# Centred weights and in-place gates in a four-layer graph network kernel on one Trainium2 core

## The chip, the cores and the metric

The kernel runs on one core of one Trainium2 chip. The metric is the device time of one execution in microseconds (us); the time of a version is the median over its runs. The profile is one execution on the same chip, seen by the hardware profiler. The engines of the core are TensorE (matmuls, called PE in the profile, its weight loads PEld), VectorE (DVE), ScalarE (ACT), GpSimd (POOL) and SyncE (SP), which issues the transfers. PSUM, into which TensorE writes, has eight banks of 128 partitions by 512 float32 values.

## The reference

The input x is 64 x 256 x 128 (batch, node, channel), the adjacency matrix `adj` is 256 x 256; everything is float32. Four layers follow one another, each with a residual and a layer norm without learned scale:

```python
x = _layernorm(x + L0(x))      # sum over k of adj^k x W_k, seven weights, adj given twice
x = _layernorm(x + L1(x))      # adj (x W1) + b1
x = _layernorm(x + L2(x))      # (A_norm x) W2^T + b2, A_norm the normalised adj + I
x = _layernorm(x + L3(x))      # five steps of a gated recurrent unit over the graph

# one step of L3, with h starting as x and in_matrix = out_matrix = adj
m = adj @ h;  av = concat(m, m);  u3 = h @ u3_w.T + u3_b
z = sigmoid(av @ w3_w.T + w3_b + u3)
r = sigmoid(av @ w4_w.T + w4_b + u3)
hv = tanh(av @ w5_w.T + w5_b + (r * h) @ u5_w.T + u5_b)
h = (1 - z) * h + z * hv

# _layernorm(x): (x - mean(x)) / sqrt(var(x) + 1e-5), over the 128 channels
```

## The kernel before

The batch is cut into 32 groups of two (`NB` = 2, L15). A group's values are tiles of 128 partitions by 512 columns: two batch elements times two halves of the nodes times 128 channels. `Group.record` (L648 to L758) writes down what a group does, operation by operation, and nothing is run there: each operation goes into a plan with an engine, an estimated cost, a lag until its result is seen, a rank and the values that it reads and writes. `Plan.order` (L83) then plays the plan through with these estimates. At every step each engine offers the operation that could start first (ties go to the lower rank, that is the earlier group), and the earliest of these offers is placed. Buffers belong to this game: a value takes a slot of its kind when its first operation is placed, and gives it back when its last one has ended. Eight PSUM banks are one such kind (`BANKS` = 8, L24). The resulting list is emitted as it is, so every engine works through a fixed order, and waits on the chip where an operand is late. At most eight groups are in flight (`ACTIVE` = 8), since a group's first operation waits for the last one of the eighth before it.

One-time work is put into the plan by `pre`: the transposed adjacency `aT`, its square, the weights. The four weights of layer 0 are summed from seven by VectorE (`w0_sums`, L277; the identity is added to the first for the residual), `w1s`, `b1s` and `b2s` are loaded as they are (L352 to L356), and `transposed` (L364) turns the 128x128 weights on TensorE and copies them out of PSUM on ScalarE.

A group goes through these stages:

- Layer 0: x times the squared adjacency (`propagate`, L672), products with the summed weights into two banks `py0`, `v` copied out, `aT` times `v` added, the sum copied to SBUF by ScalarE as `s0` (L699).
- A norm: `statistics` (L455) takes bn_stats and bn_aggr and two small scalings on VectorE (L461 to L468), the power and one product on GpSimd (L471, L472), and `normalise` (L484) applies scale and bias in four ScalarE instructions (L489).
- Layers 1 and 2: GpSimd adds the bias to the residual (`yb`, L711), `propagate` multiplies with the adjacency, a weight product goes into `py`, VectorE adds `yb` (L481), and the norm follows.
- Layer 3, five steps (L729): `propagate`, then the products of m and of hT with the gate weights. `pr` is the bank of the gates r and z: u3 hT + w4 m gives r, and w34 m added later turns the same bank into the pre-activation of z. `ph` is the bank of the candidate: w5 m + u5 (r hT). ScalarE does the gates (`gate_`, L636), VectorE does rh, d = hv - hT, e = z d and hT + e (`tensor`, L643), then a transpose and a round trip through DRAM bring h back into the other layout (`packed`, L616).
- The last residual and norm 3, then the output. The last four groups take the transpose on TensorE (L754 to L756).

`propagate` for a full group is the scheme `seven` (L510): seven block products in place of eight, with three subtractions on GpSimd before (L531 to L538), a copy on ScalarE in between (L572) and four additions on VectorE (L559 to L569) whose results gate the later block products of TensorE, since these overwrite parts of the bank that the additions read.

All matmuls are recorded under the helper at L198, all plain VectorE operations of a step under L645. Float32 matmuls are split in two instructions by the compiler, so a product counts as x2 in the profile.

Of the kernel before, what the change touches and what calls it, by code (L numbers as in the profile page):

```python
# [9 lines left out]
AF = mybir.ActivationFunctionType  # L10
OP = mybir.AluOpType
AX = mybir.AxisListType

P = 128
# [8 lines left out]
EPS = 1e-5  # L23
# [120 lines left out]
def pe_cost(columns, n=1):  # L144
    return n * 2 * (max(columns, P) / 1.2 + 2)
# [6 lines left out]
def act_cost(elements):  # L152
    return elements / 1.2 + 165
# [3 lines left out]
def kernel(  # L157
# [30 lines left out]
    nc = tc.nc  # L188
    B, N, C = x.shape
# [7 lines left out]
    def mm(o, lhsT, rhs, start, stop, shared=False):  # L197
        nc.tensor.matmul(o, lhsT, rhs, start=start, stop=stop, skip_group_check=shared)  # L198
# [7 lines left out]
    def constant(name, shape):  # L206
        v = Val("const", shape, name)
        v.tile = const.tile(shape, F32, name=name)
        return v

    def temp(name):
        return Val("bank", SHAPES["bank"], name)

    def pre(rank, engine, cost, run, reads=(), writes=()):
        lag = {"SP": 2300, "PE": 260, "DVE": 260, "ACT": 130, "POOL": 100}[engine]
        plan.add(engine, cost, lag, rank, run, reads, writes)

    def load(rank, name, shape, src, keep=True):
        v = constant(name, shape) if keep else Val("w", shape, name)
        pre(rank, "SP", 450, lambda: nc.sync.dma_start(v.ap, src), [], [v])  # L220
        return v

    ident = const.tile([P, P], F32, name="ident")
    make_identity(nc, ident)
    half = const.tile([P, Q], F32, name="half")
# [18 lines left out]
    aT, a2T = constant("aT", [P, T, N]), constant("a2T", [P, T, N])  # L244
# [30 lines left out]
    w0s = constant("w0s", [P, 4, C])  # L275
# [6 lines left out]
    pre(-7, "DVE", 1300, w0_sums, [w0_raw], [w0s])  # L282


    w0p = constant("w0p", [P, 2, C])

    def permuted():
# [15 lines left out]
    ahat, anT = Val("w", [P, T, N], "ahat"), constant("anT", [P, T, N])  # L303
# [27 lines left out]
    def block_sums(rank, name, aTs):  # L331
# [3 lines left out]
        def run():  # L335
# [13 lines left out]

    w1s = load(1.3, "w1s", [P, C], w1)  # L352
    b1s = load(1.4, "b1s", [P, C], bass.AP(tensor=b1.tensor, offset=b1.offset, ap=[[0, P], [1, C]]))
    raw = {name: load(1.5, f"raw_{name}", [P, src.shape[1]], src, False)
           for name, src in (("w2", w2), ("w4", w4_w), ("w3", w3_w), ("w5", w5_w), ("u3", u3_w), ("u5", u5_w))}
    b2s = load(1.5, "b2s", [P, C], bass.AP(tensor=b2.tensor, offset=b2.offset, ap=[[0, P], [1, C]]))  # L356
    both = {name: Val("w", [P, C], f"both_{name}") for name in ("w4", "w3", "w5", "w34")}
    for name in ("w4", "w3", "w5"):
        pre(0.4, "DVE", 220, lambda o=both[name], i=raw[name]: nc.vector.tensor_add(
# [1 line left out]
    pre(0.4, "DVE", 220, lambda: nc.vector.tensor_sub(both["w34"].ap, both["w3"].ap, both["w4"].ap),  # L361
        [both["w3"], both["w4"]], [both["w34"]])

    def transposed(name, *parts_):  # L364
        ps, v = temp(f"p_{name}"), constant(name, [P, len(parts_) * P])

        def run():
            for i, src in enumerate(parts_):
                nc.tensor.transpose(ps.ap[:, i * P:(i + 1) * P], src.ap, ident)

        n = len(parts_) * P
        pre(0.4, "PE", len(parts_) * 110, run, parts_, [ps])
        pre(0.4, "ACT", act_cost(n), lambda: nc.scalar.copy(v.ap, ps.ap[:, :n]), [ps], [v])
        return [(v, v.ap[:, i * P:(i + 1) * P]) for i in range(len(parts_))]

    w2T, u3T = transposed("w2u3T", raw["w2"], raw["u3"])
    w4T, w34T, w5T, u5T = transposed("w435u5T", both["w4"], both["w34"], both["w5"], raw["u5"])

# [8 lines left out]
    zb, rb, hb = ((bsum, bsum.ap[:, i:i + 1]) for i in range(3))  # L387


    def nat(v):  # L390
        return v.ap.rearrange("p (q c) -> p q c", c=C)
# [21 lines left out]
    class Group:  # L413
# [41 lines left out]
        def statistics(self, tag, s):  # L455
            st, mv, ve, rs, nm = (self.val(k, n + tag) for k, n in (
                ("st", "st"), ("mv", "mv"), ("ve", "ve"), ("rs", "rs"), ("ve", "nm")))

            def stats():
                for q in range(self.q):  # L460
                    nc.vector.bn_stats(st.ap[:, q * 6:(q + 1) * 6], nat(s)[:, q, :])  # L461

            def aggr():
                for q in range(self.q):
                    nc.vector.bn_aggr(mv.ap[:, 2 * q:2 * q + 2], st.ap[:, q * 6:(q + 1) * 6])
                mean, var = (mv.ap.rearrange("p (q k) -> p k q", k=2)[:, k] for k in range(2))
                nc.vector.tensor_scalar(ve.ap, var, EPS, None, op0=OP.add)
                nc.vector.tensor_scalar(nm.ap, mean, -1.0, None, op0=OP.mult)  # L468

            def scales():  # L470
                nc.gpsimd.tensor_tensor(rs.ap, ve.ap, half[:, :self.q], op=OP.pow)  # L471
                nc.gpsimd.tensor_tensor(mv.ap[:, :self.q], nm.ap, rs.ap, op=OP.mult)  # L472

            self.dve(stats, [s], [st], 195 * self.q)
            self.dve(aggr, [st], [mv, ve, nm], 67 * self.q + 240)
            self.add("POOL", 1420, 100, scales, [ve, nm], [rs, mv])
            return mv, rs

        def residual(self, tag, ps, resid, left=lambda v: v.ap, right=lambda v: v.ap):
            s = self.val("w", "s" + tag)  # L480
# [152 lines left out]
        def product(self, ps, w, rhs, start, stop, shared=False):  # L633
            self.pe(pe_cost(self.width), lambda: mm(ps.ap, w[1], rhs.ap, start, stop, shared), [rhs, w[0]], [ps])

        def gate_(self, name, ps, func, bias):  # L636
            t = self.val("w", name)
            self.act(lambda: nc.scalar.activation(t.ap, ps.ap, func, bias=bias[1], scale=1.0),  # L638
                     [ps, bias[0]], [t],
                     act_cost(self.width) + 100)  # L640
            return t
# [6 lines left out]
        def record(self):  # L648
# [24 lines left out]
            v, s0 = self.val("w", "v"), self.val("w", "s0")  # L673
            py = []
# [16 lines left out]
            for t in range(T):  # L691
# [9 lines left out]

                self.pe(pe_cost(self.nb * C, T), second, [v, aT], [py[t]])
                self.act(summed, [py[t]], [s0], act_cost(self.nb * C))
            y = self.normalise("0", s0, *self.statistics("0", s0))


            for tag, ats, w, bias in (("1", aT, (w1s, w1s.ap), b1s), ("2", anT, w2T, b2s)):
                yb = self.val("w", "yb" + tag)

                def biased(yb=yb, y=y, bias=bias):  # L710
                    nc.gpsimd.tensor_tensor(nat(yb), nat(y), bias.ap[:, None, :].to_broadcast([P, self.q, C]),  # L711
                                            op=OP.add)

                self.add("POOL", 40 + 625 * self.nb, 100, biased, [y, bias], [yb])
                m = self.propagate(tag, y, ats)
                py = self.val("bank", "py" + tag)

                def weight(py=py, m=m, w=w):
                    for q in range(self.q):
                        mm(py.ap[:, q * P:(q + 1) * P], m.ap[:, q * P:(q + 1) * P], w[1], True, True)  # L720

                self.pe(pe_cost(P, self.q), weight, [m, w[0]], [py])
                y = self.normalise(tag, *self.residual(tag, py, yb))


            h = y
            hT = self.brought("hT", self.turned("h", h, "p (q k j) -> p q k j", "p (k q i) -> p q k i"))
            ats, ins = aT, None
            for s in range(STEPS):  # L729
                m = self.propagate(f"g{s}", h, ats, ins, True)  # L730
                pr = self.val("bank", f"pr{s}")
                self.product(pr, u3T, hT, True, False)
                self.product(pr, w4T, m, False, True)
                r = self.gate_(f"r{s}", pr, AF.Sigmoid, rb)
                rh = self.tensor(f"rh{s}", OP.mult, r, hT)
                ph = self.val("bank", f"ph{s}")
                self.product(ph, w5T, m, True, False)
                self.product(pr, w34T, m, False, True, shared=True)
                z = self.gate_(f"z{s}", pr, AF.Sigmoid, zb)
                self.product(ph, u5T, rh, False, True)  # L740
                hv = self.gate_(f"hv{s}", ph, AF.Tanh, hb)

                d = self.tensor(f"d{s}", OP.subtract, hv, hT)
                e = self.tensor(f"e{s}", OP.mult, z, d)
                if s < STEPS - 1:
                    hT = self.tensor(f"hT{s}", OP.add, hT, e)
                    h, ats, ins = self.packed(f"h{s}", hT), aTp, pairs
            if self.start < B - END:
                hT = self.tensor("hT", OP.add, hT, e)
# [75 lines left out]
```

## Time and profile before

The time is 1392.04 us, the median of three runs (1391.99 to 1392.26); the profiled execution has a span of 1389.6 us. Busy time, share and number of instructions of each engine are in the first part of the profile's page. What matters around the change, from the page's groups of instructions (busy time is the union of their spans, mean is that of one instruction):

| group | count | busy us | mean ns |
|---|---|---|---|
| products of m with w4 and w34 into pr (PE, 128x512) | 640 | 325.0 | 597 |
| products of hT with u3 into pr (PE, 128x512) | 320 | 163.4 | 598 |
| bn_stats (DVE L461) | 512 | 110.5 | 275 |
| bn_aggr (DVE L465) | 512 | 46.7 | 151 |
| small scalings of a norm (DVE L467, L468) | 128 each | 32.2, 21.5 | 252, 168 |
| power of a norm (POOL L471) | 128 | 143.7 | 1123 |
| product of a norm (POOL L472) | 128 | 33.9 | 265 |
| normalise (ACT L489) | 512 | 210.6 | 483 |
| r, z, hv (ACT L638) | 160 each | 109.6, 109.5, 109.2 | 685 |
| rh, d, e, hT (DVE L645) | 160 each | 125.9, 122.5, 121.4, 125.6 | 787, 766, 761, 788 |
| residual add of layers 1 and 2 (DVE L481) | 64 | 43.5 | 679 |

A line of a group gives the program line, engine and operation, then output <- inputs by the program's names with buffer numbers left out, the shapes and the count. A line of the waits gives who waited, for whom, and in all how many us, how often, and the longest. A line of the timeline gives the start, the duration, the engine and the operation. A line of the stage table gives, for a stretch of the span, the busy us and the number of instructions of PE, PEld, DVE, ACT and POOL, then the clock that TensorE was granted (1.00 is full), the share of the transfer engines and GB/s.

### The profile page before, as it was taken

To read this page: it belongs to the slowest core of one execution; us is meant where nothing else is said; L and a number is where in the kernel's file an instruction comes from. 1 tells how busy PE (TensorE), PEld (TensorE's weight loads), DVE (VectorE), ACT (ScalarE), POOL (GpSimd) and SP (SyncE) were. 2 spreads that over 40 slices of the span, in tenths; PEclk is the share of its full clock that TensorE was granted. 3 is DMA by queue.
4 is the path that set the end of the run, shared out by engine and by line. 5 is a ranking of instruction groups with operands and counts; after the bars stand their busy time and mean duration, and the time that the engine had idled before them with its cause. 6 is when DMAs were issued, how large, how long until landed. Compare 5 with 4: busy or idle time off the path is not lost.

```text
span 1389.6 us, 22166 instructions
## 1 busy us (share of the span) xinstructions
PE 1347.1 (97%) x6516; PEld 928.3 (67%) x6516; DVE 1114.0 (80%) x3288; ACT 691.1 (50%) x1638; POOL 754.7 (54%) x1089
## 2 busy tenths in 40 slices
PE   8999999999999999999999999999999999899996
PEld 7976656676666766666577775666766667665663
DVE  5678779788887798888778798788888777988776
ACT  3554445455454445545455554544555444554444
POOL 4776526475564474754267575636655435853332
PEclk9999999999999999999999999999999999999998
DMA  6112225333343342433433323343333332133232
GB/s 190 33 54 84 84 69 167 100 98 100 91 115 91 101 113 72 131 88 117 117 87 104 93 77 91 92 128 101 91 115 107 91 90 71 52 124 104 87 91 61
DMA packets 269672, 134.45 MB, mean 97 GB/s; under 512 B 176368, under 2 KB 241392, under 8 KB 269552
## 3 DMA queue, kind: packets, MB, share of 16 engines
q1 hardware_dynamic: 269552, 133.03, 33.0%
q8 instruction: 53, 0.87, 0.3%
q14 instruction: 67, 0.55, 0.1%
HBM read 67.05 MB, written 65.54 MB: 95 GB/s over the span
## 4 chain that ended last, share of the span: by engine, by line
PE 82%; DVE 13%; issue 2%; ACT 2%; DMA 1%; SPq 1%; DVEq 0%; POOL 0%; ACTq 0%; POOLq 0%
PE pr L198 27%; PE ph L198 18%; PE pmg L198 16%; PE py L198 13%; PE pm L198 6%; PE pmq L198 2%; DVE hT L645 2%; DVE d L645 2%; DVE e L645 2%; DVE st L461 1%; DVE s L481 1%; DMA x<-in_x_dram 1%; DVE rh L645 1%; ACT hv L638 1%; DVE th L620 1%
## 5 line engine op out<-in xcount | busy, mean ns | idle before, releaser
L198 PE MATMUL pr<-mg,w435u5T 128*128 128x512 f32 x640 | 325.0, 597 | 2.3 <-DVE mg L569 2.2
L471 POOL TENSOR_TENSOR rs<-ve,half 128x4 f32<-128x4 f32 x128 | 143.7, 1123 | 232.8 <-DVE nm L468 230.7
L531 POOL TENSOR_TENSOR tsg<-h 128x256 f32<-128x256 f32 x128 | 105.2, 822 | 253.5 <-DMA h<-dh 187.6
L489 ACT ACTIVATE y<-s,mv,rs 128x128 f32<-128x128 f32 x512 | 210.6, 483 | 44.1 <-POOL mv L472 42.7
L638 ACT ACTIVATE z<-pr,bsum 128x512 f32<-128x512 f32 x160 | 109.5, 685 | 127.2 <-PE pr L198 125.0
L645 DVE TENSOR_TENSOR rh<-r,hT 128x512 f32<-128x512 f32 x160 | 125.9, 787 | 53.7 <-ACT r L638 52.8
L198 PE MATMUL pr<-hT,w2u3T 128*128 128x512 f32 x320 | 163.4, 598 | 4.2 <-DVE hT L645 3.3
L645 DVE TENSOR_TENSOR d<-hv,hT 128x512 f32<-128x512 f32 x160 | 122.5, 766 | 55.0 <-ACT hv L638 54.2
L198 PE MATMUL ph<-rh,w435u5T 128*128 128x512 f32 x320 | 163.5, 596 | 2.0 <-DVE rh L645 1.9
L638 ACT ACTIVATE r<-pr,bsum 128x512 f32<-128x512 f32 x160 | 109.6, 685 | 109.4 <-PE pr L198 109.1
L198 PE MATMUL ph<-mg,w435u5T 128*128 128x512 f32 x320 | 163.6, 593 | 0.0
L198 PEld LDWEIGHTS pr<-mg,w435u5T 128*128 128x128 f32 x640 | 110.2, 191 | 76.9 <-issue 59.1
L638 ACT ACTIVATE hv<-ph,bsum 128x512 f32<-128x512 f32 x160 | 109.2, 685 | 48.5 <-PE ph L198 47.9
L645 DVE TENSOR_TENSOR hT<-hT,e 128x512 f32<-128x512 f32 x160 | 125.6, 788 | 1.4
L198 PEld LDWEIGHTS pmg<-aTp,h 128*128 128x128 f32 x512 | 88.6, 197 | 52.7 <-issue 38.3
L198 PEld LDWEIGHTS pmg<-s_aTp,tsg 128*128 128x128 f32 x768 | 101.8, 191 | 32.2 <-issue 26.1
L645 DVE TENSOR_TENSOR e<-z,d 128x512 f32<-128x512 f32 x160 | 121.4, 761 | 1.4
L461 DVE BATCH_NORM_STATS2 st<-s 128x6 f32<-128x128 f32 x512 | 110.5, 275 | 3.6 <-ACT s L699 3.0
L198 PE MATMUL pmg<-s_aTp,tsg 128*128 128x128 f32 x768 | 106.5, 275 | 0.2 <-POOL tsg L535 0.2
L581 ACT COPY mg<-pmg 128x128 f32<-128x128 f32 x160 | 42.3, 264 | 121.6 <-PE pmg L198 90.4
L198 PE MATMUL pmg<-aTp,h 128*128 128x128 f32 x512 | 98.7, 280 | 0.5 <-DVE mq L569 0.3
L198 PEld LDWEIGHTS ph<-mg,w435u5T 128*128 128x128 f32 x320 | 58.0, 192 | 57.4 <-issue 41.6
(159 smaller groups left out, 2686.6 us busy)
## 6 DMA issues: line engine op xcount, KB each, us to landing
dh<-th SPq DMA_DIRECT2D x160, 256.0 KB, 2.0
h<-dh SPq DMA_DIRECT2D x256, 128.0 KB, 2.5
x<-in_x_dram SPq DMA_DIRECT2D x32, 256.0 KB, 3.4
hT<-dh SPq DMA_DIRECT2D x128, 64.0 KB, 2.0
out_dram<-y SPq DMA_DIRECT2D x32, 256.0 KB, 2.4
dx<-tx SPq DMA_DIRECT2D x30, 256.0 KB, 2.6
xT<-dx SPq DMA_DIRECT2D x60, 128.0 KB, 2.6
dn<-tn SPq DMA_DIRECT2D x28, 256.0 KB, 2.0
```

What stands on the lines that cost most here:

```text
L198: nc.tensor.matmul(o, lhsT, rhs, start=start, stop=stop, skip_group_check=shared)
L461: nc.vector.bn_stats(st.ap[:, q * 6:(q + 1) * 6], nat(s)[:, q, :])
L471: nc.gpsimd.tensor_tensor(rs.ap, ve.ap, half[:, :self.q], op=OP.pow)
L481: self.dve(lambda: nc.vector.tensor_add(right(s), left(ps), right(resid)), [ps, resid], [s])
L489: nc.scalar.activation(nat(y)[:, q, :], nat(s)[:, q, :], AF.Identity, bias=mv.ap[:, q:q + 1], scale=rs.ap[:, q:q + 1])
L531: nc.gpsimd.tensor_tensor(ts.ap[:, :2 * P].rearrange("p (x c) -> p x c", x=2), ins(h)[:, 1], ins(h)[:, :, 0], op=OP.subtract)
L581: self.act(lambda: nc.scalar.copy(o(m, 0), o(ps, 0, False)), [ps], [m], act_cost(P), True)
L620: self.dve(lambda: nc.vector.transpose(turn.ap.rearrange("p (u j t) -> p u t j", t=T, j=32), src.ap.rearrange("p (u t i) -> p u t i", t=T, ...
L638: self.act(lambda: nc.scalar.activation(t.ap, ps.ap, func, bias=bias[1], scale=1.0), [ps, bias[0]], [t], act_cost(self.width) + 100)
L645: self.dve(lambda: nc.vector.tensor_tensor(out(t), way(a), way(b), op=op), [a, b], [t])
```

## The change

Layers 0 to 2 end in sums whose mean over the channels is to be zero, so that their norms need no mean. For that, each weight has the mean over its output channels taken out once, at the start: the summed weights of layer 0 with the identity (`centre(w0s, w0m)`), w1, b1 and b2 (put together in one tile `wb`), and w2, whose transpose on TensorE becomes a product with the identity less 1/128 everywhere (`less`). The residual that layers 1 and 2 add is a norm's output, which has mean zero already. These norms are then: ScalarE squares and sums the row with its accumulator output (the factor 1/128 sits in the scale), GpSimd adds epsilon and takes the power, and one VectorE multiply with the row factors broadcast gives the output. Norm 3 stays as it was.

In layer 3, z and tanh are written in place into their PSUM banks `pr` and `ph` instead of to SBUF, and d and e read them there. The product of w4 with m is the first one into `pr`, and that of u3 with hT the second.

```diff
+    def centre(v, means):
+        nc.vector.reduce_sum(means.ap, v.ap, axis=AX.X)
+        nc.vector.tensor_scalar(means.ap, means.ap, -1.0 / C, None, op0=OP.mult)
+        nc.vector.tensor_tensor(v.ap, v.ap, means.ap[:, :, None].to_broadcast(v.ap.shape), op=OP.add)
+
+    w0m = constant("w0m", [P, 4])
+    pre(-7, "DVE", 1500, lambda: centre(w0s, w0m), [w0s], [w0s, w0m])
...
-    w1s = load(1.3, "w1s", [P, C], w1)
-    b1s = load(1.4, "b1s", [P, C], bass.AP(tensor=b1.tensor, offset=b1.offset, ap=[[0, P], [1, C]]))
+    wb, wbm = constant("wb", [P, 3, C]), constant("wbm", [P, 3])
+    pre(1.3, "SP", 450, lambda: nc.sync.dma_start(wb.ap[:, 0, :], w1), [], [wb])
+    for i, b in ((1, b1), (2, b2)):
+        pre(1.4, "SP", 450, lambda i=i, b=b: nc.sync.dma_start(
+            wb.ap[:, i, :], bass.AP(tensor=b.tensor, offset=b.offset, ap=[[0, P], [1, C]])), [wb], [wb])
+    pre(0.35, "DVE", 1100, lambda: centre(wb, wbm), [wb], [wb, wbm])
...
+    less = constant("less", [P, P])
+    pre(0.4, "DVE", 200, lambda: nc.vector.tensor_scalar(less.ap, ident, -1.0 / C, None, op0=OP.add), [], [less])
...
-                nc.tensor.transpose(ps.ap[:, i * P:(i + 1) * P], src.ap, ident)
+                if src is raw["w2"]:
+                    mm(ps.ap[:, i * P:(i + 1) * P], src.ap, less.ap, True, True)
+                else:
+                    nc.tensor.transpose(ps.ap[:, i * P:(i + 1) * P], src.ap, ident)
...
+            def squares():
+                for q in range(self.q):
+                    nc.scalar.activation(nat(y)[:, q, :], nat(s)[:, q, :], AF.Square, scale=C ** -0.5,
+                                         accum_out=ve.ap[:, q:q + 1])
+
+            def scales():
+                nc.gpsimd.tensor_scalar(ve.ap, ve.ap, EPS, None, op0=OP.add)
+                nc.gpsimd.tensor_tensor(rs.ap, ve.ap, half[:, :self.q], op=OP.pow)
+
+            self.act(squares, [s], [y, ve], 400 * self.q)
+            self.add("POOL", 1330, 100, scales, [ve], [ve, rs])
+            return y, rs
+
+        def normalise_centred(self, tag, s):
+            y, rs = self.spread_of(tag, s)
+            self.dve(lambda: nc.vector.tensor_tensor(nat(y), nat(s), rs.ap[:, :, None].to_broadcast([P, self.q, C]),
+                                                     op=OP.mult), [s, rs], [y])
+            return y
...
-            t = self.val("w", name)
+            t = self.val("w", name) if kept else ps
...
-            y = self.normalise("0", s0, *self.statistics("0", s0))
+            y = self.normalise_centred("0", s0)
...
-                y = self.normalise(tag, *self.residual(tag, py, yb))
+                y = self.normalise_centred(tag, self.added(tag, py, yb))
...
-                self.product(pr, u3T, hT, True, False)
-                self.product(pr, w4T, m, False, True)
+                self.product(pr, w4T, m, True, False)
+                self.product(pr, u3T, hT, False, True)
...
-                z = self.gate_(f"z{s}", pr, AF.Sigmoid, zb)
+                z = self.gate_(f"z{s}", pr, AF.Sigmoid, zb, False)
                 self.product(ph, u5T, rh, False, True)
-                hv = self.gate_(f"hv{s}", ph, AF.Tanh, hb)
+                hv = self.gate_(f"hv{s}", ph, AF.Tanh, hb, False)
```

More of the change, by code (lines that the diff above doesn't have):

```diff
@@ L348 @@
     block_sums(0.7, "aTp", aTp)
-    w1s = load(1.3, "w1s", [P, C], w1)
-    b1s = load(1.4, "b1s", [P, C], bass.AP(tensor=b1.tensor, offset=b1.offset, ap=[[0, P], [1, C]]))
+    wb, wbm = constant("wb", [P, 3, C]), constant("wbm", [P, 3])
[4 more added lines that the diff above has]
+    pre(0.35, "DVE", 1100, lambda: centre(wb, wbm), [wb], [wb, wbm])
+    w1c, b1c, b2c = ((wb, wb.ap[:, i, :]) for i in range(3))
     raw = {name: load(1.5, f"raw_{name}", [P, src.shape[1]], src, False)
            for name, src in (("w2", w2), ("w4", w4_w), ("w3", w3_w), ("w5", w5_w), ("u3", u3_w), ("u5", u5_w))}
-    b2s = load(1.5, "b2s", [P, C], bass.AP(tensor=b2.tensor, offset=b2.offset, ap=[[0, P], [1, C]]))
     both = {name: Val("w", [P, C], f"both_{name}") for name in ("w4", "w3", "w5", "w34")}
@@ L368, in run @@
             for i, src in enumerate(parts_):
-                nc.tensor.transpose(ps.ap[:, i * P:(i + 1) * P], src.ap, ident)
+                if src is raw["w2"]:
+                    mm(ps.ap[:, i * P:(i + 1) * P], src.ap, less.ap, True, True)
+                else:
+                    nc.tensor.transpose(ps.ap[:, i * P:(i + 1) * P], src.ap, ident)
         n = len(parts_) * P
-        pre(0.4, "PE", len(parts_) * 110, run, parts_, [ps])
+        pre(0.4, "PE", len(parts_) * 110, run, [*parts_, less], [ps])
         pre(0.4, "ACT", act_cost(n), lambda: nc.scalar.copy(v.ap, ps.ap[:, :n]), [ps], [v])
@@ L477, in statistics, with spread_of, added @@
             return mv, rs
+        def spread_of(self, tag, s):
+            y, ve, rs = self.val("w", "y" + tag), self.val("ve", "ve" + tag), self.val("rs", "rs" + tag)
+            def squares():
[13 more added lines that the diff above has]
+            return y
+        def added(self, tag, ps, resid):
+            s = self.val("w", "s" + tag)
+            self.dve(lambda: nc.vector.tensor_add(s.ap, ps.ap, resid.ap), [ps, resid], [s])
+            return s
         def residual(self, tag, ps, resid, left=lambda v: v.ap, right=lambda v: v.ap):
@@ L634, in product, with gate_ @@
             self.pe(pe_cost(self.width), lambda: mm(ps.ap, w[1], rhs.ap, start, stop, shared), [rhs, w[0]], [ps])
-        def gate_(self, name, ps, func, bias):
-            t = self.val("w", name)
+        def gate_(self, name, ps, func, bias, kept=True):
+            t = self.val("w", name) if kept else ps
             self.act(lambda: nc.scalar.activation(t.ap, ps.ap, func, bias=bias[1], scale=1.0),
@@ L703, in record @@
                 self.act(summed, [py[t]], [s0], act_cost(self.nb * C))
-            y = self.normalise("0", s0, *self.statistics("0", s0))
-            for tag, ats, w, bias in (("1", aT, (w1s, w1s.ap), b1s), ("2", anT, w2T, b2s)):
+            y = self.normalise_centred("0", s0)
+            for tag, ats, w, bias in (("1", aT, w1c, b1c), ("2", anT, w2T, b2c)):
                 yb = self.val("w", "yb" + tag)
                 def biased(yb=yb, y=y, bias=bias):
-                    nc.gpsimd.tensor_tensor(nat(yb), nat(y), bias.ap[:, None, :].to_broadcast([P, self.q, C]),
+                    nc.gpsimd.tensor_tensor(nat(yb), nat(y), bias[1][:, None, :].to_broadcast([P, self.q, C]),
                                             op=OP.add)
-                self.add("POOL", 40 + 625 * self.nb, 100, biased, [y, bias], [yb])
+                self.add("POOL", 40 + 625 * self.nb, 100, biased, [y, bias[0]], [yb])
                 m = self.propagate(tag, y, ats)
```

## The prediction

> **What bounds the kernel now.** I read the page's busy times and its chain of waits first, then the waits of the matmul queue, then the matmuls in order of time, and last the groups of VectorE and ScalarE. The page's first and fourth parts:
>
> ```profile
> PE 1347.1 (97%) x6516; PEld 928.3 (67%) x6516; DVE 1114.0 (80%) x3288; ACT 691.1 (50%) x1638; POOL 754.7 (54%) x1089
> ...
> PE 82%; DVE 13%; issue 2%; ACT 2%; DMA 1%; SPq 1%; DVEq 0%; POOL 0%; ACTq 0%; POOLq 0%
> ```
>
> TensorE (PE) is the bound, and what is on the chain beside it is VectorE (DVE). But 97% overstates it, because the shown end of a matmul overlaps the next one. The timeline around 607 us shows how fast full-width products really follow each other:
>
> ```profile
> 607.33 1.02 PE L198 MATMUL ph<-mg,w435u5T 128*128 128x512 f32 x2
> 608.19 1.02 PE L198 MATMUL pr<-mg,w435u5T 128*128 128x512 f32 x2
> 609.04 1.02 PE L198 MATMUL ph<-rh,w435u5T 128*128 128x512 f32 x2
> ```
>
> A pair is shown as 1.02 us and the next pair starts after 0.855, so one 512-wide matmul takes 0.4277 us of the array. In the same way 256-wide ones are 0.2165 apart (36.01, 36.45, 36.88) and 128-wide ones 0.1105. Then PE's own work is 1600 x 0.4277 + 792 x 0.2165 + 4124 x 0.1105 = 684 + 171 + 456 = 1311 us. Walking the matmul starts with these spacings, PE stands still for 59.5 us: 9.1 in the first 50 us, 44.6 between 50 and 1350, 5.8 after that. The other 19 us of the span are 9 after the last matmul and some 10 of slower clock and small gaps. The change touches no matmul count, so only these 78 us can move, and the middle 44.6 are the prize. The waits of the matmul queue say who ends them:
>
> ```profile
> PE pth L591 <- DVE hT L645: 5.2, 2, 4.6
> PE pmg L198 <- DVE mg L565: 5.2, 8, 2.1
> PE pr L198 <- DVE hT L645: 3.3, 6, 1.2
> PE py L198 <- DVE m L569: 2.8, 2, 1.8
> PE pm L198 <- DVE m L565: 2.6, 2, 2.2
> PE pmq L198 <- DMA x<-in_x_dram: 2.4, 2, 1.3
> PE pr L198 <- DVE mg L569: 2.2, 6, 0.6
> ```
>
> Except for the start's x transfer it is VectorE every time: an operation that PE needs stands late in VectorE's queue. The stalls come in clumps, as the stage table shows; where they clump the clock also drops to 0.97:
>
> ```profile
> 300.00:350.00 50.00, 47.93 (x230) 32.07 (x229) 41.82 (x123) 25.62 (x60) 29.59 (x43) 0.97 0.32 92
> 1000.00:1050.00 50.00, 50.00 (x242) 34.56 (x241) 42.43 (x118) 26.48 (x63) 28.67 (x38) 1.00 0.30 90
> 1200.00:1250.00 50.00, 45.98 (x231) 31.57 (x231) 45.48 (x161) 27.62 (x66) 31.29 (x48) 0.97 0.33 106
> ```
>
> **What the skill says.** (1) The Trainium skill, "SBUF — State Buffer", Who interferes with whom: a VectorE instruction with two SBUF inputs contends with a GpSimd instruction that reads SBUF, one with at most one SBUF input does not. The trace agrees: the lines of residual adds and of gate differences (min/median/max ns) are
>
> ```profile
> L481 DVE TENSOR_TENSOR s<-py,yb x64: 645/680/693, 43.5 to 1226.3; 128x512 f32<-128x512 f32 x64
> L645 DVE TENSOR_TENSOR d<-hv,hT x160: 639/692/1598, 84.4 to 1377.5; 128x512 f32<-128x512 f32 x160
> ```
>
> The add with one PSUM input never exceeds 693 ns; the difference with two SBUF inputs reaches 1598. (2) "ScalarE: Activation LUTs", What happens when an `exp` ACTIVATE runs: PSUM is the lower-latency destination for ScalarE. No row before writes PSUM from ScalarE. (3) The same page, What ACT_TABLE_LOAD costs: 186 ns plus 0.833 per element, 93 ns for each pointer operand, back to back 93 less. For the present normalise (two pointers, 128 elements) that gives 479 and a spacing of 386; the trace has 483 and 210.6/512 = 411.
>
> **The change, part by part.**
>
> *Norms 0 to 2 (96 of 128).* Removed from VectorE, as three quarters of the rows' busy time: bn_stats 110.5, aggregates 46.7, the two small scalings 32.2 and 21.5, together 210.9 x 0.75 = 158 us. Added: 96 multiplies of 128x512 with two SBUF inputs, 0.775 each (the rows rh, hT, d and e have 761 to 788) = 74. Net -84 us. ScalarE loses 0.75 x 210.6 = 158 us and gets 384 squares. From below, one pointer operand and a free accumulator: 0.30 each by the page's price; from above, the accumulator as a second instruction with the fixed 186 ns again and less overlap: 0.60. So 115 to 230; I take 0.45 = 173. ScalarE then stands at 650 to 765 us, 47 to 55% of the span: not the bound. GpSimd swaps a 265 ns multiply for an addition on the same 128x4: nothing.
>
> *z and tanh left in PSUM (L645's d and e).* Both now have one PSUM input, so 0.679 as for the add above: 122.5 + 121.4 - 2 x 160 x 0.679 = -27 us. ScalarE's two gates take 685 or somewhat less. Together VectorE goes from 1114 to about 1004 us.
>
> *A new wait.* The multiply stands in VectorE's queue and waits for GpSimd's power; until now it was ScalarE's normalise that waited there (42.7 us over 128 norms, 38 times). If VectorE inherits it, 0.75 x 42.7 = 32 us are blocked, and queued behind are the additions of the seven-product scheme (L559 to L569), for which PE waits. Counting it as load: (1004 + 32)/1375 = 75% against 80%.
>
> *Banks.* From the mean times of opening and closing, pr is held for 17.8 us now (from u3's product to the end of z) and ph for 4.95. Opened by w4's product some 13 us later (about 739.2 against 726.3) and kept to the end of e (748.1, instead of 744.1), pr is held for 9; ph, kept to the end of d, for 6. In mean banks: pr 2.05 to 1.03, ph 0.57 to 0.69, and all kinds together 5.75 to 4.85 of 8. Room is gained even though two values stay longer.
>
> *u3 after w4.* The same two products, but both are now behind m and before r: 0.86 us more on the chain of each step, and 160 x 0.86 = 138 us of PE work that could fill a gap before m was there now cannot. Eight groups are in flight, with 5.8 us of PE work a step each, so in the middle it is hidden behind other groups' products; at the end I charge 1 us.
>
> *The start.* Centring w0 adds three VectorE instructions (0.69 for a 128x512 reduction, 0.17, 0.7) before the first use of w0s at 14.19 us; w0s is ready at 8.9 us, so up to 5 us of slack hides it. Centring b1, b2 and w1 likewise lies before 30.9 us, where b1 is first read. The w2 transpose becomes a matmul of the same width. The tail keeps the old norm 3. I charge 1 us.
>
> *Sum.* If stalls behind a queue grow as load/(1 - load), 80.2% gives 4.05 and 75.3% gives 3.05, a quarter less: 44.6 x 0.25 = -11. Fewer clumps: -2 of clock. Banks: -3, the stalls that no VectorE operation ends (2.1 on "issue", 0.9 on tanh). Start and end +2. In all -14: 1392 - 14 = 1378 us.
>
> **The rivals.** *A, 55%: as summed, 1378*, with some 12 either way, since the planner writes a new order from new costs. *B, 18%: nothing to speak of, 1389.* For it: stall and VectorE load go badly together in the stage table (42.43 busy without stall, 41.82 with 4 us), so the written order, not the load, may set the stalls; then only the clock and a few waits of banks move. Against: the waits name VectorE. *C, 17%: slower, 1402.* The fill work of u3 is gone, the inherited wait blocks the additions, and ScalarE at the upper bound delays its copies: a tenth of 138 us unfilled is +14, half of the 32 us blocked would reach PE as +16, less the -15 to -20 of lighter VectorE and banks: +10. If Square were not in the table in use, loads would come with each norm and this case would be worse; the trace shows one load for sigmoid, tanh, copy and identity. *D, 10%: nearly all middle stalls go, 1350*: 1392 - 40 - 2. For it: contention falls too, and with it the long rows of 1.6 us that start clumps.
>
> **How the numbers follow.** 1378 is A's. The range runs from D's to C's, 1350 to 1403; it leaves out the worse half of C and a little below D. Faster by over 0.2% (below 1389.3): nearly all of A, D, half of B = 0.72; within: 0.08; slower: C and the rest of B = 0.20.
>
> **What would show it.** Right: VectorE near 1005 us busy, d and e at 0.68 with no row over 0.75, fewer waits of PE on hT and L565, no window at 0.97, pr open for about 9 us. Wrong: more than one table load; squares over 0.6 apart; long waits of the new multiply on GpSimd with waits of PE on L559 to L569 behind them; waits of PE on w4's or u3's operands that are longer than now.

## The result and the profile after

The changed kernel takes 1370.02 us (median of 4 runs, 1369.68 to 1371.42) against 1392.15 us of the kernel before in the same session: a ratio of 0.9842, 95% interval 0.9825 to 0.9859. That is 22.1 us less, where 14 were forecast; the time lies in the range. (The kernel before is run again beside each change, so its median differs a little from one comparison to the next.) The profiled span fell from 1389.6 to 1367.9 us.

The engines' busy times and the chain of waits of the changed kernel, to be held against the first two lines that the prediction shows:

```profile
PE 1340.5 (98%) x6517; PEld 926.0 (68%) x6517; DVE 1021.9 (75%) x2431; ACT 650.7 (48%) x2022; POOL 720.4 (53%) x1089
...
PE 91%; DVE 5%; DMA 1%; ACT 1%; issue 1%; POOL 1%; SPq 0%; DVEq 0%; ACTq 0%; POOLq 0%
```

TensorE's share of the chain rose from 82 to 91% and VectorE's fell from 13 to 5%. VectorE is busy 92 us less, ScalarE 40 us less, GpSimd 34 us less. TensorE's own work is the same: with the spacings of the prediction it is 1311.6 us, against 1311.5. Going through the matmul starts in order, and counting as standing still what lies between a start and the one before it beyond these spacings, shows where the time came from:

| TensorE stands still | before, us | after, us |
|---|---|---|
| first 50 us | 9.1 | 9.1 |
| from 50 to 1340 us | 44.6 | 22.9 |
| after that, before the last matmul | 5.8 | 5.9 |
| span left after the start of the last matmul | 8.8 | 8.6 |

The whole gain is 21.7 us of stalls in the middle. Of the 44.6 us before, some 24 are ended by VectorE in the timeline's own records; of the 22.9 after, 9.3 are. The rest mostly are short gaps without a named releaser. In the kernel before, 3.4 us of it are no waits at all but matmuls at half the clock, which the section on new orders below shows; the changed kernel has none of these in the middle. The waits of the matmul queue say the same:

```profile
PE pth L640 <- DVE mv L485: 3.5, 2, 3.2
PE pr L198 <- DVE mg L618: 2.8, 5, 1.0
PE pm L198 <- DVE m L614: 2.3, 3, 1.6
PE pmq L198 <- DMA x<-in_x_dram: 2.0, 1, 2.0
PE ph L198 <- DVE rh L695: 1.9, 4, 0.7
PE warm L238 <- POOL ident masks.py:199: 1.3, 1, 1.3
PE pmg L198 <- ACT usg L621: 0.9, 2, 0.5
```

The waits for `hT` before u3's product (3.3 us) are gone, those for the third addition of the seven-product scheme in layer 3 (`mg` L565 before, 5.2 us) are nearly gone; the wait of the last transpose belongs to the tail and stays. In the stage table the clumps at these places and the two middle windows at clock 0.97 are gone too (the largest idle share in the middle is now 2.7 us, from 1150 to 1200 us); the same three stretches now read

```profile
300.00:350.00 50.00, 49.87 (x261) 36.83 (x260) 34.85 (x87) 23.57 (x80) 30.92 (x49) 1.00 0.33 95
...
1000.00:1050.00 50.00, 49.93 (x231) 34.15 (x230) 38.47 (x97) 22.03 (x68) 32.53 (x50) 1.00 0.37 107
...
1200.00:1250.00 50.00, 48.63 (x198) 28.35 (x198) 39.60 (x95) 23.39 (x53) 15.43 (x25) 1.00 0.36 104
```

d and e, which read tanh and z from PSUM, have lost their long rows, and the new multiply `y`, with two SBUF inputs, has them (min/median/max ns):

```profile
L695 DVE TENSOR_TENSOR d<-ph,hT x160: 644/691/694, 84.5 to 1355.5; 128x512 f32<-128x512 f32 x160
L695 DVE TENSOR_TENSOR e<-pr,d x160: 644/684/693, 85.3 to 1356.7; 128x512 f32<-128x512 f32 x160
L519 DVE TENSOR_TENSOR y<-s,rs x96: 643/691/1774, 28.1 to 1206.2; 128x512 f32<-128x512 f32 x96
```

ScalarE's rows of the new norm and of the two gates in place (count, then busy us and mean ns) are

```profile
L505 ACT ACTIVATE y<-s 128x128 f32<-128x128 f32 x384 | 113.7, 301 | 24.0 <-DVE s L525 23.6
...
L688 ACT ACTIVATE pr<-pr,bsum 128x512 f32<-128x512 f32 x160 | 105.6, 660 | 117.7 <-PE pr L198 114.9 <-DVE d L695 1.1 <-DVE th L669 1.0
L688 ACT ACTIVATE ph<-ph,bsum 128x512 f32<-128x512 f32 x160 | 105.5, 659 | 63.3 <-PE ph L198 62.3 <-DVE mg L618 0.6
L505 ACT ACTIVATION_READ_ACCUMULATOR y<-s 128x1 f32 x384 | 73.2, 191 | 0.0
```

The sum comes out by an instruction of its own, 191 ns, so a square with its sum takes (113.7 + 73.2)/384 = 0.487 us of ScalarE.

### The profile page after: what moved, and what is told of

Same layout as the page of the kernel before. It is cut to its first block, busy times and chain, and to the rows that moved or that the text cites. A ratio compares the mean times of both kernels' runs of the same rounds, so it can differ in the third digit from the quotient of the medians.

```text
span 1367.9 us, 21546 instructions
## 1 busy us (share of the span) xinstructions
PE 1340.5 (98%) x6517; PEld 926.0 (68%) x6517; DVE 1021.9 (75%) x2431; ACT 650.7 (48%) x2022; POOL 720.4 (53%) x1089
## 4 chain that ended last, share of the span: by engine, by line
PE 91%; DVE 5%; DMA 1%; ACT 1%; issue 1%; POOL 1%; SPq 0%; DVEq 0%; ACTq 0%; POOLq 0%
PE pr L198 29%; PE ph L198 19%; PE pmg L198 18%; PE py L198 15%; PE pm L198 6%; PE pmq L198 3%; DVE rh L695 1%; DVE st L481 0%; DMA w_raw<-in_L_gnn_weight_dram 0%; DVE d L695 0%; DVE e L695 0%; DVE s L530 0%; DVE hT L695 0%; ACT r L688 0%; DVE y L519 0%
## 5 line engine op out<-in xcount | busy, mean ns | idle before, releaser
L580 POOL TENSOR_TENSOR tsg<-h 128x256 f32<-128x256 f32 x128 | 102.4, 800 | 256.2 <-DMA h<-dh 157.6
L695 DVE TENSOR_TENSOR d<-ph,hT 128x512 f32<-128x512 f32 x160 | 109.6, 685 | 71.3 <-ACT ph L688 70.4
L688 ACT ACTIVATE pr<-pr,bsum 128x512 f32<-128x512 f32 x160 | 105.6, 660 | 117.7 <-PE pr L198 114.9
L688 ACT ACTIVATE ph<-ph,bsum 128x512 f32<-128x512 f32 x160 | 105.5, 659 | 63.3 <-PE ph L198 62.3
L505 ACT ACTIVATE y<-s 128x128 f32<-128x128 f32 x384 | 113.7, 301 | 24.0 <-DVE s L525 23.6
L695 DVE TENSOR_TENSOR hT<-hT,e 128x512 f32<-128x512 f32 x160 | 119.4, 749 | 1.2
L491 POOL TENSOR_TENSOR rs<-ve,half 128x4 f32<-128x4 f32 x32 | 34.5, 1079 | 151.2 <-DVE nm L488 151.0
L695 DVE TENSOR_TENSOR e<-pr,d 128x512 f32<-128x512 f32 x160 | 108.9, 682 | 1.3
L510 POOL TENSOR_TENSOR rs<-ve,half 128x4 f32<-128x4 f32 x96 | 102.0, 1063 | 8.0
L618 DVE TENSOR_TENSOR mg<-pmg,usg 128x256 f32<-128x256 f32 x160 | 66.8, 418 | 46.4 <-PE pmg L198 45.3
L761 POOL TENSOR_TENSOR yb<-y,wb 128x512 f32<-128x512 f32 x64 | 86.7, 1357 | 26.9 <-DVE y L519 26.9
```

The lines of the kernel that those rows point to most:

```text
L505: nc.scalar.activation(nat(y)[:, q, :], nat(s)[:, q, :], AF.Square, scale=C ** -0.5, accum_out=ve.ap[:, q:q + 1])
L580: nc.gpsimd.tensor_tensor(ts.ap[:, :2 * P].rearrange("p (x c) -> p x c", x=2), ins(h)[:, 1], ins(h)[:, :, 0], op=OP.subtract)
L618: nc.vector.tensor_tensor(o(m, slice(1, 3)), o(ps, slice(1, 3), False), both, op=OP.add)
L695: self.dve(lambda: nc.vector.tensor_tensor(out(t), way(a), way(b), op=op), [a, b], [t])
L761: nc.gpsimd.tensor_tensor(nat(yb), nat(y), bias[1][:, None, :].to_broadcast([P, self.q, C]), op=OP.add)
```

## The experiments

Three theories stand against each other. **Load**: TensorE's middle stalls follow VectorE's load, so what counts is how much work VectorE is spared. **Banks**: what counts is the PSUM room from opening `pr` by w4's product. **Order**: the planner writes a new order for every change, and this one happened to fall well. All ratios are to the kernel before, run beside each kernel (its medians were 1390.4 to 1391.4 us); the changed kernel's own ratio is 0.9842.

### The same order, with VectorE's load put back

```diff
+    idle = const.tile([P, Q * 6], F32, name="idle")
...
+            def multiplied():
+                nc.vector.tensor_tensor(nat(y), nat(s), rs.ap[:, :, None].to_broadcast([P, self.q, C]), op=OP.mult)
+                for q in range(self.q):
+                    nc.vector.bn_stats(idle[:, q * 6:(q + 1) * 6], nat(s)[:, q, :])
+
+            self.dve(multiplied, [s, rs], [y])
```

The plan's costs are untouched, so every engine runs the changed kernel's instructions in the changed kernel's order (the two traces agree in this instruction by instruction), with 384 bn_stats more on VectorE.

> The changed kernel with every engine's order kept as it is, but with four bn_stats more behind each of the 96 multiplies of norms 0 to 2, whose output nobody reads (the outputs of the kernel are the same). VectorE gets back 96 x 4 x 0.216 = 83 us, so its load returns to about 1105 us. Load theory (the stalls of TensorE follow VectorE's load; the change took 92 us from VectorE and 21 us from the middle stalls, 0.23 us for each): about 1389 us. Bank theory (the gain is PSUM room, from opening pr by w4's product): below 1375. Order theory (each new plan falls out differently, and this one fell well): below 1375, since the order is the same.

Measured: 1389.47 us, ratio 0.9989 (0.9983 to 0.9995). The busy times and the added group in this kernel:

```profile
PE 1347.6 (97%) x6517; PEld 926.4 (67%) x6517; DVE 1086.3 (78%) x2815; ACT 649.9 (47%) x2022; POOL 717.9 (52%) x1089
```

```profile
L523 DVE BATCH_NORM_STATS2 idle<-s 128x6 f32<-128x128 f32 x384 | 82.7, 275 | 0.0
```

82.7 us of idle work on VectorE, 64 in its busy time, cost 19.4 us, with every order, bank and buffer the same. The middle stalls went from 22.9 to 41.9 us, none of them at a lowered clock. GpSimd is as busy as in the changed kernel (718 us against 720), and the readers of `y` don't wait for the idle work: GpSimd's addition to `y` (L761) starts 0.28 us after the multiply's end in the median of both kernels. So it is the operations queued behind that come late. The load theory named 1389 and the other two below 1375. This is the main finding: VectorE work of about the size that the change takes away has a price of the size of the gain. The idle work stands in 96 blocks behind the multiplies, not where the removed work stood; that the same load costs the same in other places isn't shown.

### The same order, with the gates' results in SBUF

```diff
-            t = self.val("w", name) if kept else ps
+            t = self.val("w", name)
...
-                     [ps, bias[0]], [t],
+                     [ps, bias[0]], [t] if kept else [t, ps],
...
-                d = self.tensor(f"d{s}", OP.subtract, hv, hT)
-                e = self.tensor(f"e{s}", OP.mult, z, d)
+                d = self.tensor(f"d{s}", OP.subtract, hv, hT, held=[ph])
+                e = self.tensor(f"e{s}", OP.mult, z, d, held=[pr])
```

The plan believes the banks to be held as in the changed kernel, so the order is the same instruction by instruction, as the traces confirm.

> The changed kernel with z and tanh written to SBUF again, but the plan told that their banks stay held until d and e have ended, so that every engine keeps its order. Only d and e change: two SBUF inputs, which meet GpSimd's reads. Load theory: VectorE gets some 25 us more and rows beyond 1 us, about 1376 us. Bank and order theory: 1370 within 2.

Measured: 1382.61 us, ratio 0.9939 (0.9923 to 0.9955). The busy times and the row of d:

```profile
PE 1345.8 (97%) x6517; PEld 927.7 (67%) x6517; DVE 1052.3 (76%) x2431; ACT 657.4 (48%) x2022; POOL 772.1 (56%) x1089
```

```profile
L695 DVE TENSOR_TENSOR d<-hv,hT x160: 642/692/1767, 86.9 to 1368.7; 128x512 f32<-128x512 f32 x160
```

The long rows are back, and 12.6 us with them, about twice what VectorE's load alone led me to expect. The load theory has the sign; what it lacked is the other side of the meeting: GpSimd, which does the same operations in both kernels, is busy 52 us longer (720.4 against 772.1). Its middle subtraction of layer 3, in the changed kernel first and in this one second, takes 547 and 640 ns in the mean:

```profile
L584 POOL TENSOR_TENSOR tsg<-h,tsg 128x128 f32<-128x128 f32 x128 | 69.8, 547 | 5.9
...
L584 POOL TENSOR_TENSOR tsg<-h,tsg 128x128 f32<-128x128 f32 x128 | 81.7, 640 | 5.9
```

So two SBUF inputs in d and e slow both engines that feed TensorE, and waits of TensorE for a GpSimd subtraction now appear (1.1 us). ScalarE's two gates are some 25 ns longer each as well, since they write to SBUF. How the 12.6 us divide between the three engines wasn't separated. In the profiled execution 2.4 us of the difference stand in the first 50 us, where TensorE waits 3.3 us for x instead of 2.0, and 10.9 in the middle.

### One part taken out of the changed kernel

Each of these three lets the planner write a new order. (Where the old norms are put back, here and below, the weights stay centred.)

```diff
-            y = self.normalise_centred("0", s0)
+            y = self.normalise("0", s0, *self.statistics("0", s0))
...
-                y = self.normalise_centred(tag, self.added(tag, py, yb))
+                y = self.normalise(tag, *self.residual(tag, py, yb))
```

> The changed kernel with the old norm (bn_stats, aggregates, four scalings on ScalarE) in layers 0 to 2; the weights stay centred. VectorE gets back some 70 us. Load theory: 1370 + 0.23 x 70 = 1386 us. Bank theory: 1370 to 1374. Order theory: anywhere from 1365 to 1395.

```diff
-                z = self.gate_(f"z{s}", pr, AF.Sigmoid, zb, False)
+                z = self.gate_(f"z{s}", pr, AF.Sigmoid, zb)
...
-                hv = self.gate_(f"hv{s}", ph, AF.Tanh, hb, False)
+                hv = self.gate_(f"hv{s}", ph, AF.Tanh, hb)
```

> The changed kernel with z and tanh in SBUF as before, so that the plan gives pr and ph back early and writes its own order. Against the run with the gates in SBUF and the order kept (1382.6), this one has more room in PSUM and VectorE the same work. Load theory: 1380 to 1385, the same as with the order kept. Bank theory: below 1376, as pr is held 5 us less. Order theory: anywhere from 1365 to 1395.

```diff
-                self.product(pr, w4T, m, True, False)
-                self.product(pr, u3T, hT, False, True)
+                self.product(pr, u3T, hT, True, False)
+                self.product(pr, w4T, m, False, True)
```

> The changed kernel with u3's product opening pr again, before m is there; with z left in place pr is then held for some 22 us. Bank theory: 1385 or more. Load theory: 1370 within 3, as VectorE's work is the same. Order theory: anywhere from 1365 to 1395.

| taken out | us | ratio (95% interval) | VectorE busy us |
|---|---|---|---|
| new norms | 1382.37 | 0.9935 (0.9918 to 0.9952) | 1077.6 |
| gates in PSUM | 1381.98 | 0.9932 (0.9919 to 0.9944) | 1056.6 |
| w4's product first | 1383.15 | 0.9939 (0.9926 to 0.9953) | 1027.3 |

Each costs 12 to 13 us. For the norms and the gates that fits the load theory (1386 and 1380 to 1385 were expected), and the gates give the same 1382 with the order kept or not. The third does not fit it: VectorE's work is nearly that of the changed kernel, and the time is still 13 us more. It could be banks, or order. The order theory had allowed 1365 to 1395 for each, so these three say nothing against it.

### One part alone in the kernel before

The same three edits, two at a time, leave one part alone.

> The kernel before with the centred weights and new norms alone (gates in SBUF, u3 first). VectorE loses some 70 us. Load theory: 1392 - 0.23 x 70 = 1376 us. Bank theory: 1390 to 1393, as pr is held for 17.8 us still. Order theory: anywhere from 1370 to 1395.

> The kernel before with z and tanh left in PSUM alone (old norms, u3 first). VectorE loses some 27 us and the long rows of d and e go, pr is held for some 22 us. Load theory: 1384 us. Bank theory: 1395 or more, since pr takes 2.5 banks of 8 in the mean instead of 2.05. Order theory: anywhere from 1370 to 1400.

> The kernel before with w4's product first into pr alone (old norms, gates in SBUF). VectorE's work is as before, pr is held for some 5 us instead of 17.8. Load theory: 1390 to 1393 us. Bank theory: 1378 to 1384. Order theory: anywhere from 1370 to 1400.

| alone | us | ratio (95% interval) | VectorE busy us |
|---|---|---|---|
| new norms | 1389.47 | 0.9990 (0.9982 to 0.9997) | 1064.3 |
| gates in PSUM | 1387.13 | 0.9971 (0.9965 to 0.9978) | 1078.0 |
| w4's product first | 1387.88 | 0.9975 (0.9968 to 0.9982) | 1102.4 |

None fits the load theory or the bank theory well; all lie within the wide ranges of the order theory. The norms alone should have given 1376 by load and give 1389, though VectorE falls by 50 us (GpSimd rises by 22, from 754.7 to 776.4); that is near the bank theory's 1390. The gates alone are faster where the bank theory wanted 1395, although pr is held longest there; w4 alone gives half of the least that banks promised. The three gains, 0.10 + 0.29 + 0.25%, make 0.64%, and all together give 1.58%. So either the parts help each other, or a new order is worth so much that single runs with new orders can't be read to within 10 us. The next runs measure that.

### How much a new order alone is worth

```diff
-            return self.add("DVE", cost or dve_cost(self.width), 260, run, reads, writes, joint)
+            return self.add("DVE", cost or dve_cost(self.width), 261, run, reads, writes, joint)
```

> The changed kernel with one number of the plan moved by a nanosecond: the lag after a VectorE operation is 261 instead of 260. The work of every engine, the buffers and the banks are as they are; some 40% of TensorE's order is written otherwise. Load theory: 1370 within 3. Order theory (the changed kernel's order fell well by 8 to 12 us, which is what the parts alone don't add up to): 1376 to 1385.

The same line with 270, in the kernel before:

> The kernel before with the lag after a VectorE operation set to 270 instead of 260 in the plan; the same work in a new order. Load theory: 1391 within 3. Order theory: anywhere from 1380 to 1400, which would give the width of what a new order alone does.

```diff
-            self.act(squares, [s], [y, ve], 400 * self.q)
+            self.act(squares, [s], [y, ve], 487 * self.q)
...
-                                                     op=OP.mult), [s, rs], [y])
+                                                     op=OP.mult), [s, rs], [y], 830)
```

> The changed kernel with two estimates of the plan set to what its profile shows: four squares with their accumulator reads 487 ns each instead of 400, the multiply 830 instead of 645. The work is the same, the order is new. If a truer plan stalls less: below 1370. Load theory: 1370 within 3. Order theory: 1376 to 1385.

```diff
-BANKS = 8
+BANKS = 7
```

> The changed kernel with seven PSUM banks in the plan in place of eight, which takes back about the 0.9 bank that the later opening of pr gives in the mean. Bank theory: 1380 or more. Load theory: 1370 within 3. Order theory: 1376 to 1385, like any new order.

| new order | us | ratio (95% interval) | VectorE busy us |
|---|---|---|---|
| changed, lag 261 | 1377.68 | 0.9904 (0.9887 to 0.9922) | 1029.6 |
| changed, truer costs | 1376.75 | 0.9898 (0.9883 to 0.9914) | 1017.8 |
| changed, seven banks | 1372.65 | 0.9873 (0.9858 to 0.9889) | 1025.5 |
| before, lag 270 | 1397.07 | 1.0041 (1.0029 to 1.0054) | 1105.3 |

A nanosecond in one estimate moves the time by nearly 8 us, with the same work on every engine. The busy times of that run differ from the changed kernel's by less than 1%:

```profile
PE 1343.2 (98%) x6517; PEld 926.6 (67%) x6517; DVE 1029.6 (75%) x2431; ACT 649.7 (47%) x2022; POOL 718.8 (52%) x1089
```

So the order theory is right about a part: this order is the best of four that I have of the changed kernel, and the order of the kernel before is the better of two. It is not what makes the gain as a whole: the four changed ones (1370 to 1378) and the two of before (1391 and 1397) don't touch, and their means, 1374 and 1394, are 20 us apart. Truer costs did not make a better plan.

A part of what an order does is the clock. In the profiled execution of the kernel before, TensorE's granted clock is halved twice in the middle, each time for 3.4 us and each time just after a stall of about 2 us that VectorE ended. There two 128-wide matmuls take 0.43 us, where the prediction's spacing gives 0.22:

```profile
325.28 0.50 PE L198 MATMUL pmg<-s_aTp,h 128*128 128x128 f32 x2 [2.07 <-DVE mg L565]
...
326.43 0.64 PE L198 MATMUL pm<-s_aT,y 128*128 128x128 f32 x2
326.86 0.64 PE L198 MATMUL pm<-s_aT,tq 128*128 128x128 f32 x2
...
326.20:329.40 3.20, 3.20 (x10) 2.10 (x9) 2.01 (x6) 1.54 (x6) 2.84 (x6) 0.50 0.28 82
1203.40:1206.60 3.20, 3.20 (x13) 2.56 (x12) 3.17 (x17) 1.75 (x5) 2.19 (x4) 0.50 0.29 85
```

By the spacings these two cost 3.4 us. The same kernel with lag 270 has 17 us of such stretches in the middle, which cost 7.2 of its 49.2 us of middle stalls; without them both orders stand still for 41 to 42 us, so nearly all of what parts their two traces is clock. In the run with w4's product first alone they cost 4.7 of 41.1 us, so its waits fell by more than its time shows, to some 36 us. The changed kernel, the one with idle work, lag 261 and seven banks have none in the middle. Other stalls of 2 us in the kernel before (at 193.5 and 514.1 us) are not followed by a lower clock, so what sets it off isn't shown.

Seven banks cost no more than any new order does, and less than the other two. Each engine's records stand in the plan's order, so every bank value can be followed through a trace, from its first matmul to its last reader: the mean number of banks taken is 6.0 in the kernel before, 6.1 in the changed one and 5.5 in the changed one with seven. So the room that pr gave back is taken by other values at once (the banks of layer 0's `pmq` are held for 44.5 us in the mean instead of 32.7), and with seven banks fewer are free, 1.5, than the kernel before had with eight, 2.0. The changed kernel isn't short of banks, and the mean room doesn't explain the gain. That the kernels with u3 first met moments of shortage is not excluded by this.

### All runs together

The eight combinations of the three parts are complete, and each part can be read in four pairs that differ in it alone:

| part | change of the ratio in the four pairs, % | mean, % | in us |
|---|---|---|---|
| new norms | -0.10, -0.32, -0.43, -0.93 | -0.45 | -6.2 |
| gates in PSUM | -0.29, -0.51, -0.40, -0.90 | -0.53 | -7.3 |
| w4's product first | -0.25, -0.58, -0.36, -0.97 | -0.54 | -7.5 |

(First the pair without the other two parts, last the pair with both.) All twelve have one sign. With 3 to 4 us of scatter for a new order, a mean over four pairs is good to about 2.5 us, so each part is worth something and they can't be ranked. The largest step of each row ends at the one order of the changed kernel that fell best; with one of its other orders, at 0.990, the last steps would be -0.3 to -0.4, like the rest, which leaves no sign that the parts help each other.

Over all 14 kernels, which have the same TensorE work, a straight-line fit of the time against VectorE's busy time and whether w4 comes first gives 0.16 us (standard error 0.03) for each us of VectorE and -5.3 us (1.9) for w4 first, and leaves 3.1 us of scatter. Read with it, the change is 92 x 0.16 = 15 us of VectorE load, 5 us of w4 first, and 1 to 2 us of order and rest. The fit is a summary and no proof, since contention makes VectorE's busy time an effect as well as a cause; what shows that load on VectorE is a cause is the pair with one and the same order, where the price was 19.4/64 = 0.30 us for each us of busy time. How the 22 us divide between the parts is an estimate. Why w4 first helps at equal load was not settled: it frees banks, and it also puts u3's product elsewhere in the order, and no run parts these two.

## Why the prediction was right, point by point

**The bound and the prize.** Right. TensorE's work did not move, the start and the tail did not either, and all of the gain is in the 44.6 us of middle stalls, of which VectorE ended more than half.

**VectorE's load.** The rows are right: the sums by group went down by 109.6 us, 111 were forecast (d and e by 12.9 + 12.5 for 27, the norms by 159 for 158; the multiply took 80 us where I had 74, its rows being stretched to 835 ns in the mean; rh and hT became 8 us shorter together, and the centring added 3). The total that I made of it, 1004 us, was wrong by 18: I subtracted busy times of groups from the page's busy time, but neighbouring VectorE instructions overlap there (the groups of before add up to 1251 us, those of after to 1142; the page has 1114 and 1022). Removing many short instructions removes less from the page than from the groups.

**The price of the load.** This is the term that was mis-sized. I took a quarter off the stalls by load/(1 - load), which is 11 us, and the runs with one order show 19.4 us for 64 us of busy time (0.30 a us); 92 us at that price would be 28, more than the whole gain; by the fit over all kernels they are 15. The direction and the place were right, the queueing formula was too weak: by a third against the fit, by more against the pair.

**The clock.** 2 us were forecast from fewer clumps. The two stretches at half clock in the middle, 3.4 us, are gone; one of the same length (3.4 us, so 1.7 lost) now stands in the first 50 us, at 25.7 us, and the stalls there stayed at 9.1 us.

**The new wait.** Smaller than charged: the multiply waited 20.6 us for GpSimd where 32 were assumed, and only one wait of TensorE on the multiply shows, of 0.3 us.

```profile
DVE y L519 <- POOL rs L510: 20.6, 24, 2.3
```

**ScalarE.** The squares took 187 us, inside 115 to 230 and near the 173 taken. The Trainium skill, "ScalarE: Activation LUTs", What ACT_TABLE_LOAD costs, gives an estimate of 186 + 107 = 293 ns for an instruction without pointer operands, and the row has 301: no pointer was charged here. The accumulator's read was the second instruction that my upper end assumed. Writing the gates to PSUM saved 25 ns of 685, which agrees with what the same page, What happens when an `exp` ACTIVATE runs, says of PSUM as the lower-latency destination.

**Contention.** The Trainium skill, "SBUF — State Buffer", Who interferes with whom, has VectorE with two SBUF inputs and a reading GpSimd contend, and I took that into VectorE's rows and left it out for GpSimd. The run with the gates in SBUF and the order kept agrees and shows that half: 52 us of GpSimd.

**Banks.** The holding times came out near the forecast: pr for 10.7 us (9 forecast, 18 before), ph for 7.6 (6). The step from there to room, 5.75 to 4.85 banks, was wrong: other values filled it, and the mean went from 6.0 to 6.1. I booked 3 us for the room and 1 us against w4 first for the lost fill work. The runs give w4 first 5 to 7.5 us, so its sign as a whole was right and its size too small; whether banks are its cause stays open, and a net loss by the missing fill work showed in none of the four pairs.

**Start and end.** Charged 2 us; the stalls show nothing of it (9.1 and 9.1, 5.8 and 5.9). The centring was hidden, as worked out, and I should have booked it at zero.

**The rivals.** B, that the written order sets the stalls and VectorE's load does not matter, was wrong in its conclusion and right in its ground: a new order moves the time by 3 to 8 us. C falls: one table load, no stalls behind the multiply. D's full relief did not come; 22.9 us of middle stalls are left.

**Luck.** The time lies 8 us under the 1378 named. Some of that is this one order: the other three of the changed kernel gave 1372.7 to 1377.7 us, and the mean of all four is 4 us above it. The sum of the parts also came near with one of its terms too small (load) and one without support (room).

## What to carry to other kernels

In a kernel bound by TensorE, price work on the engine that feeds it by the stalls it causes: here 0.16 (the fit) to 0.30 us (one order, work added) of kernel for each us of VectorE at 75 to 80% load, and 12.6 us for 30 where two engines were meeting at SBUF. Before reading a part's effect from one run with a replanned order, disturb the plan by a nanosecond and see how far the time moves, and look at the granted clock of short stretches; to test a cause, keep the order and add idle work. Where a value has a PSUM bank already and one VectorE reader more, leaving it there can be cheaper than SBUF, as it was here.

## What the runs showed of the hardware that I had not expected

A VectorE operation with one input in PSUM was not only free of stretched rows itself (694 ns at most in 160 rows of d, against 1767 with both in SBUF); a subtraction of GpSimd was shortened as well, from 640 to 547 ns in the mean, and the kernel was 12.6 us faster by this one placement with the order unchanged. The granted clock of TensorE fell to half in stretches of 3.4 us, twice in the middle of the kernel before, each time within 0.9 us after a stall of 2 us. The sum over a row by ScalarE's accumulator cost 191 ns beyond the 301 of the square of 128 elements.
